# Two approximate 3x3 convolutions: channels ranked on chip, and softmax maxima in layer 2 for 3 of 11 channel groups

## The chip, the core and the metric

The kernel runs on one core of one Trainium2 chip. The metric is device microseconds of one execution. Before the change the median of three runs is 3927.82 us (3924.66 to 3930.93). One more execution was profiled. The engines are called as in the profile: PE is TensorE (PEld its weight loads), DVE is VectorE, ACT ScalarE, POOL GpSimd, SP SyncE.

## The reference

The input is 16 images of 256 channels with 28x28 pixels, all in fp32. For every image:

```python
g = group_norm(x)                       # 32 groups of 8 channels
h = relu(bn1(amm_conv3x3(g, centroids1, wsub1)))
y = bn2(amm_conv3x3(h, centroids2, wsub2))
y = y * sigmoid(relu(mean(y) @ se_w1 + se_b1) @ se_w2 + se_b2)
out = x + relu(y + g)

def amm_conv3x3(x, centroids, w_sub):   # centroids (256,16,9), w_sub (256,9,256)
    p = 3x3 patches of each channel                    # (b, n, c, s), s = 9
    d = sum(p*p) - 2 * einsum('bncs,cks->bnck', p, centroids) + sum(centroids**2)
    attn = softmax(-d, over the 16 codes k)
    lut = einsum('cks,cso->cko', centroids, w_sub)
    return einsum('bnck,cko->bno', attn, lut)
```

Each channel's 3x3 patch is softly replaced by a mix of 16 codes of nine numbers, and the mix, over all channels, goes through an ordinary product with `w_sub`. The term `p*p` is the same for all 16 codes and drops out of the softmax. What is left, the logit, is `2pc - cc`. In exact arithmetic the softmax doesn't depend on whether the largest logit is taken off ahead of the exponential; in fp32 a logit that is too large overflows, and a channel whose logits are all very negative loses its sum.

## The kernel before

**Tiling.** The 256 channels lie three to a *row tile* of 32 rows (9 patch rows each, and rows for other uses): 84 row tiles hold three channels, and four hold one of the last four each. Four row tiles fill the 128 partitions, and eight (two halves `h`) make one of 11 *groups*. Groups 9 and 10 come first, since their numbers are dealt out into spare rows of the other nine (`qx`, L503). The 784 pixels of an image are taken in two parts of 384 and 400. One group and one part is a *slot*: 22 slots make a *stage*, which is one layer of one image, and there are 32 stages in the order L1(0), L1(1), L2(0), L1(2), L2(1), and so on.

**What a slot does.** Patches `pt` come from a DRAM copy `pat` of the shifted image (L365, POOL's queue). TensorE forms 16 codes' logits for the 24 channels of the group with 16 products (L378, `wd` holds the codes and the term `cc`), ScalarE takes the exponential (L444), TensorE turns it into nine mixed numbers and one sum for each channel (L454, `cw`). VectorE turns these so that pixels lie on partitions (`nt`, L466) and takes reciprocals of the sums (`rc`, L470), POOL scales (L487, L493), VectorE turns back (`q`, L514), and TensorE forms the output products (L525, weights `ws`): 36 of 128x128 for each part, summed over nine groups in two accumulator banks. Layer 1 doesn't take maxima; it records the largest and smallest reciprocal of each slot instead (`ext`, L473 and L474).

**Maxima in layer 2.** Five slots ahead of its own, every slot of layer 2 forms the same logits once more. VectorE turns them (`z`, L397, two transposes) and takes the maximum over the 16 codes (`mx`, L405, two reductions), turns the result (`mt`, L414), and SP stores it to DRAM and loads it into four spare rows of `pt` (L423, L431), from where the later logit products subtract it. So these slots have two sets of L378 products and two DVE steps of each sort more.

**Order.** Every engine runs its instructions in the order in which they are written. The class `Plan` is a table: `at(slot, position, job)` files a job, and `emit` writes them sorted by slot and position. Within a slot the positions are: 0 logits for a maximum, 1 `z`, 2 `q`, 3 L454, 4 `nt`, `rc` and scaling, 5 logits, 6 exponential, 7 spare rows, 8 `mx`, 9 loading. A slot's own logits are in slot s, its L454 in s+1, its `q` in s+2, its output products from the fifth slot on. Output products are filed at position 1 or 7 (three or four of 36 in each slot; `early` in the code). Three pairs of PSUM banks (`pair`, 2 x 512 numbers) go around in the order of use; all logits and all L454 results share them.

**Side work** is filed into the same slots: the next image's norm on VectorE (`gn_stats` to `gn_apply`, L252 and L281), its shifted copies, the writing of the patches to DRAM (`to_pat`, L301, 15 transfers for a stage on ACT's queue), and the finish of the image before (SE gate, L351 to L353).

**The guard.** At the end the recorded reciprocals are tested. If a sum of exponentials left the range 1e-26 to 1e26 (`S_LIM`), a conditional block computes every image again with maxima in both layers.

The host only lays the arrays out (`wd`, `cw`, `ws` of both layers in row-tile order).

## Time and profile before

| | |
|---|---|
| median of three runs | 3927.82 us |
| profiled execution, its time | 3933.48 us |
| its span | 3931.8 us |
| PE busy | 91% of the span |
| DVE busy | 83% |
| ACT, POOL busy | 38%, 33% |
| mean granted clock of TensorE | 0.975 |
| chain that ended last | DVE 53%, PE 28% |

A group of the page names line, engine, operation, `out<-in` with the tiles' names, its count, its busy time and the mean of one, then the engine's idle time ahead of it and what ended most of that. A row of single instructions starts with its start time and its duration; `[1.60 <-POOL nt L487]` at its end says that the engine was idle for 1.60 us until POOL's result of line 487 came. The granted clock is TensorE's, as a share of full speed. A row of stretches gives start and end in us and, after the comma, the busy time of each engine inside it.

### The profile page before, as it was taken

The numbers are of one execution on the slowest core, as the hardware profiler recorded it, in microseconds if no ns is written. First come the engines' busy times: TensorE is split into PE (matmuls) and PEld (weight loads), VectorE is DVE, ScalarE is ACT, GpSimd is POOL, SyncE is SP. The second block draws the span as 40 slices with busy tenths as digits, with TensorE's granted clock in tenths as the row PEclk, the third lists the DMA queues.
The fourth block names the chain that finished last, engine by engine and source line by source line (L and its number), as shares of the span: only waits on it lengthen the run. The fifth ranks groups of instructions, "written<-read, shape, count | busy, mean of one in ns | idle before, by whom it ended". The sixth has DMA issues, their size and how long they took to land.

```text
span 3931.8 us, 81773 instructions
## 1 busy us (share of the span) xinstructions
PE 3570.4 (91%) x33042; PEld 1295.3 (33%) x33042; DVE 3261.3 (83%) x4710; ACT 1507.9 (38%) x2417; POOL 1283.9 (33%) x1314
## 2 busy tenths in 40 slices
...
GB/s 252 170 165 155 180 119 160 166 139 197 132 171 133 145 191 165 159 116 154 186 151 194 117 169 146 146 198 144 172 112 146 198 159 170 112 159 172 148 89 58
DMA packets 361805, 611.05 MB, mean 155 GB/s; under 512 B 205370, under 2 KB 217802, under 8 KB 361162
## 3 DMA queue, kind: packets, MB, share of 16 engines
...
HBM read 338.50 MB, written 271.94 MB: 155 GB/s over the span
## 4 chain that ended last, share of the span: by engine, by line
DVE 53%; PE 28%; issue 6%; DMA 5%; POOL 3%; ACT 2%; ACTq 2%; POOLq 0%; DVEq 0%; SPq 0%
PE acc L525 14%; DVE z L397 13%; DVE mx L405 11%; DVE nt L466 10%; DVE q L514 10%; PE pair L378 9%; DVE rc L470 5%; PE pair L454 5%; POOL nt L487 3%; ACTq L301 2%; DMA dm<-mt 1%; DMA pat<-side 1%; DVE y L352 1%; ACT y L351 1%; DVE y L353 1%
## 5 line engine op out<-in xcount | busy, mean ns | idle before, releaser
L444 ACT ACTIVATE e<-pair 128x768 f32<-128x768 f32 (+1 forms) x1408 | 1111.4, 822 | 1913.6 <-PE pair L378 1734.0
L525 PE MATMUL acc<-q,ws 128*128 128x384 f32 (+1 forms) x4608 | 1798.0, 523 | 0.0
L378 PE MATMUL pair<-pt,wd 31*64 31x400 f32 (+1 forms) x16896 | 1252.2, 519 | 246.1 <-DVE z L397 182.3
L487 POOL TENSOR_TENSOR nt<-nt,rc 128x648 f32<-128x648 f32 (+1 forms) x576 | 773.9, 1344 | 1752.5 <-DVE rc L470 1568.1
L525 PEld LDWEIGHTS acc<-q,ws 128*128 128x128 f32 x4608 | 818.4, 193 | 970.9 <-issue 582.4
L514 DVE STREAM_TRANSPOSE q<-nt 128x768 f32<-128x768 f32 (+1 forms) x576 | 569.0, 988 | 292.7 <-POOL nt L487 253.0
L466 DVE STREAM_TRANSPOSE nt<-pair 128x768 f32<-128x768 f32 (+1 forms) x704 | 688.8, 978 | 126.5 <-PE pair L454 123.6
L454 PE MATMUL pair<-e,cw 64*32 64x384 f32 (+1 forms) x11264 | 648.8, 506 | 76.0 <-DVE nt L466 61.6
L397 DVE STREAM_TRANSPOSE z<-pair 128x768 f32<-128x768 f32 (+1 forms) x704 | 665.5, 983 | 56.8 <-PE pair L378 55.6
L378 PEld LDWEIGHTS pair<-pt,wd 31*64 31x64 f32 x16896 | 310.8, 130 | 1114.9 <-DVE z L397 625.2
L405 DVE TENSOR_REDUCE mx<-z 128x48 f32<-128x768 f32 (+1 forms) x704 | 643.9, 957 | 0.0
L470 DVE RECIPROCAL rc<-nt 128x72 f32<-128x72 f32 (+1 forms) x704 | 438.2, 622 | 24.2
L365 POOL DMA_DIRECT2D pt<-pat x384 | 299.4, 780 | 446.2 <-PE pair L378 374.2
L503 ACT COPY nt<-qx 128x120 f32<-128x120 f32 (+1 forms) x576 | 183.8, 319 | 332.3 <-DVE rc L470 332.1
L493 POOL TENSOR_TENSOR qx<-nt,rc 128x324 f32<-128x324 f32 (+3 forms) x256 | 166.2, 668 | 407.7 <-DVE rc L470 396.3
L454 PEld LDWEIGHTS pair<-e,cw 64*32 64x32 f32 x11264 | 134.3, 105 | 476.8 <-issue 267.8
L352 DVE SCALAR_TENSOR_TENSOR y<-xt,gn_rstd,y 128x392 f32<-128x392 f32 x64 | 47.9, 749 | 77.6 <-ACT y L351 77.6
L473 DVE TENSOR_REDUCE ext<-rc 128x1 f32<-128x72 f32 (+1 forms) x352 | 81.3, 231 | 12.1
L414 DVE STREAM_TRANSPOSE mt<-mx 128x256 f32<-128x256 f32 x192 | 81.2, 423 | 6.5
L474 DVE TENSOR_REDUCE ext<-rc 128x1 f32<-128x72 f32 (+1 forms) x352 | 77.6, 220 | 0.0
L289 ACT COPY side<-im 128x756 f32<-128x756 f32 x64 | 52.6, 823 | 51.0 <-DMA pat<-im 35.9
L351 ACT ACTIVATE y<-y,se_nb,se_gt 128x392 f32<-128x392 f32 x64 | 45.3, 712 | 38.1 <-issue 34.3
...
## 6 DMA issues: line engine op xcount, KB each, us to landing
...
pat<-side ACTq DMA_DIRECT2D x128, 771.8 KB
...
```

Source lines behind the costliest of these rows:

```text
L365: nc.gpsimd.dma_start(pt[:, : 2 * len(gs), :n], view(u["pat"], 2 * gs[0] * P * HW + px, [[HW, P], [P * HW, 2 * len(gs)], [1, n]]),)
L378: nc.tensor.matmul(ps[i // 2][64 * h : 64 * h + 64, i % 2, :n], lhsT=wd[l][32 * i : 32 * i + rows, 2 * g + h, :], rhs=u["pt"][32 * i : 32 ...
L397: nc.vector.transpose(z[:, : 64 * nb].rearrange("p (i m) -> p i m", i=2), ps[:, :, : 32 * nb])
L405: nc.vector.tensor_reduce(u["mx"][:, a : a + 2].rearrange("p i (c b) -> p i b c", c=2)[:, :, :nb], z[:, : 64 * nb].rearrange("p (i b c k) ...
L444: nc.scalar.activation(e[:, :, :n], ps[:, :, :n], AF.Exp, scale=2.0)
L454: nc.tensor.matmul(ps[32 * i : 32 * i + 32, h, :n], lhsT=cw[l][64 * h : 64 * h + 64, g, i, :], rhs=es[i // 2][64 * h : 64 * h + 64, i % 2, ...
L466: nc.vector.transpose(t[:, : 2 * nb].rearrange("p (h b) r -> p h (b r)", h=2), u.pop(("nm", gi))[:, :, : 32 * nb])
L470: nc.vector.reciprocal(rc[:, : 2 * nb], t[:, : 2 * nb, SUM : SUM + 3])
L487: nc.gpsimd.tensor_tensor(v, v, rc[:, : 2 * nb].unsqueeze(3).to_broadcast([P, 2 * nb, 3, 9]), ALU.mult)
L503: nc.scalar.copy(u["nt", gi][0][:, : 2 * nb].rearrange("p (h b) r -> p h b r", h=2)[:, :, :, SUM:], bass.AP(w.tensor, w.offset, [list(w.ap ...
L514: nc.vector.transpose(q[:, : 64 * nb], t[:, : 2 * nb].rearrange("p b r -> p (b r)"))
L525: nc.tensor.matmul(accs[key][:, :n], lhsT=ws[l][:, 2 * g + h, o * P : (o + 1) * P], rhs=u["q", gi][:, 32 * nb * h : 32 * nb * h + n], star ...
```

## The change

The changed kernel takes maxima in layer 2 for groups 0, 3 and 6 only (`MAXED`). These three hold 72 channels, and which channels they are is found on the chip. At the start VectorE works out a key for each of the 256 channels between the layers, (5 |bn scale| + bn shift) times the largest sum of positive numbers of a code, and ranks the channels by it (`sort_channels`). The 72 highest go to the places of groups 0, 3 and 6 (`places`), the others follow. The rank makes a permutation matrix `perm`, and with it TensorE reorders all that has one entry for each of these channels: the outputs of layer 1 (`sort_bn`, `sort_ws1` in 18 blocks), and codes and weights of layer 2 (`sort_c2`, `sort_ws2` in six parts). The latter go to DRAM and from there by 86 transfers on SP's queue to their places in `wd`, `cw` and `ws` (`place_wd2`, `place_cw2`, `place_ws2`, `place_extra`). Layer 1 as computed then has its channels in sorted order, so layer 2 sees them so. All of that stands ahead of the plan's first slot.

In layer 2 the units are `MIXED`: four pairs of groups without maxima, and three single groups with them, whose patches have a pool of their own (`mpool`, three buffers; `ppool` has four instead of five). A group without maxima is treated as in layer 1, its range tests included, and its patches come four slots ahead instead of nine. Layer 2's logits are lowered by a constant 25 (`SHIFT`, through a row of ones in `pt`), and the limits of the guard become 1e-26 and 1e32. The conditional block still takes all maxima. Output products in a slot are split in two halves, position 1 and 7, where that slot has logits for a maximum, and all stand at position 7 elsewhere. The preparation of layer 2's codes (`setup_codes(1)`) moves from slot 4 to slot 18.

```diff
-S_LIM = 1e26
+S_MIN, S_MAX = 1e-26, 1e32
...
 ORDER = [9, 10] + list(range(NBG))
-UNITS = [ORDER[i : i + 2] for i in range(0, NG, 2)]
+PAIRS = [ORDER[i : i + 2] for i in range(0, NG, 2)]
+MAXED = (0, 3, 6)
+MIXED = [[9, 10], [0], [1, 2], [3], [4, 5], [6], [7, 8]]
+REACH = 5.0
+SHIFT = (0.0, 25.0)
...
+def places():
+
+    first = [rt + NFULL * j for g in MAXED for rt in range(8 * g, 8 * g + 8) for j in range(NCH)]
+    return first + [c for c in range(3 * NFULL + 4) if c not in first]
...
+    c2_sb = const.tile([P, NB, K * 9], F32, name="c2_sb")
+    nc.sync.dma_start(c2_sb, cent2.rearrange("(b p) m -> p b m", p=P))
+    sort_sb = hpool.tile([P, NB * HW], F32, tag="y", name="sort_sb")
+    n_in = sorting.shape[1]
+    nc.sync.dma_start(sort_sb[:, :n_in], sorting)
...
+    wd = [load(wd1, "wd0"), const.tile([P, NT, 64], F32, name="wd1")]
+    cw = [load(cw1, "cw0"), load(cw2, "cw1")]
+    ws = [const.tile([P, NBT, C], F32, name=f"ws{l}") for l in range(2)]
+    nc.gpsimd.memset(wd[1], 0.0)
...
-    NSTAT = B * len(PXT) * NG
+    NSTAT = B * len(PXT) * (2 * NG - len(MAXED))
...
+    def sort_channels():
+        sc, sh = bn[0]
+        key = small.tile([P, NB], F32, name="key")
+        pos = scratch(NB * K * 9)
+        nc.vector.tensor_scalar_max(pos, c2_sb.rearrange("p b m -> p (b m)"), 0.0)
+        sums = small.tile([P, NB * K], F32, name="sums")
+        nc.vector.tensor_reduce(sums, pos.rearrange("p (m s) -> p m s", s=9), axis=AX.X, op=ALU.add)
+        nc.vector.tensor_reduce(key, sums.rearrange("p (b k) -> p b k", k=K), axis=AX.X, op=ALU.max)
+        t = small.tile([P, NB], F32, name="key_t")
+        nc.vector.tensor_scalar_mul(t, sc, -1.0)
+        nc.vector.tensor_max(t, t, sc)
+        nc.vector.scalar_tensor_tensor(t, t, REACH, sh, op0=ALU.mult, op1=ALU.add)
+        nc.vector.tensor_mul(key, key, t)
+        ps = bank()
+        for b in range(NB):
+            dg = scratch(P)
+            nc.vector.tensor_scalar_mul(dg, ident, key[:, b : b + 1])
+            nc.tensor.matmul(ps[:, b * P : (b + 1) * P], lhsT=ones_sq, rhs=dg, start=True, stop=True)
+        row = scratch(C)
+        nc.vector.tensor_copy(row, ps[:, :C])
+        own = small.tile([P, NB], F32, name="key_own")
+        rank = small.tile([P, NB], F32, name="rank")
+        for b in range(NB):
+            dg = scratch(P)
+            nc.vector.tensor_mul(dg, row[:, b * P : (b + 1) * P], ident)
+            nc.vector.tensor_reduce(own[:, b : b + 1], dg, axis=AX.X, op=ALU.add)
+            gt = scratch(C)
+            eq = scratch(C)
+            nc.vector.tensor_scalar(gt, row, own[:, b : b + 1], None, op0=ALU.is_gt)
+            nc.vector.tensor_scalar(eq, row, own[:, b : b + 1], None, op0=ALU.is_equal)
+            nc.vector.tensor_mul(eq, eq, earlier[:, b])
+            nc.vector.tensor_add(gt, gt, eq)
+            nc.vector.tensor_reduce(rank[:, b : b + 1], gt, axis=AX.X, op=ALU.add)
+            nc.vector.tensor_scalar(perm[:, b], ranks, rank[:, b : b + 1], None, op0=ALU.is_equal)
...
+    PART = 384
+    def part_of(ap, i):
+        t = tpool.tile([P, 832], F32, tag="z", name="part")[:, : NB * PART].rearrange("p (b m) -> p b m", b=NB)
+        nc.sync.dma_start(t, ap[:, i * PART : (i + 1) * PART].rearrange("(b p) m -> p b m", p=P))
+        return t
+    def sort_ws1(i):
+        t = part_of(ws1, i)
+        for j in range(PART // P):
+            ps = bank()
+            for b in range(NB):
+                nc.tensor.matmul(
+                    ps[:, :C], lhsT=t[:, b, j * P : (j + 1) * P], rhs=perm[:, b], start=(b == 0), stop=(b == NB - 1)
+                )
+            nc.scalar.copy(ws[0][:, i * PART // P + j], ps[:, :C])
+    d_c2 = [dram.tile([C, K * 9], F32, name=f"dc2{i}") for i in range(2)]
+    d_ws2 = dram.tile([C, 9 * C], F32, name="dws2")
+    def by_position(ps, rhs, m):
+        for v in range(NB):
+            for b in range(NB):
+                nc.tensor.matmul(
+                    ps[:, v, :m], lhsT=perm[:, b, v * P : (v + 1) * P], rhs=rhs[:, b], start=(b == 0), stop=(b == NB - 1)
+                )
+    def sort_c2():
+        ps = pair()
+        by_position(ps, c2_sb, K * 9)
+        for i in range(2):
+            t = scratch(NB * K * 9).rearrange("p (b m) -> p b m", b=NB)
+            if i == 0:
+                nc.scalar.copy(t, ps[:, :, : K * 9])
+            else:
+                nc.scalar.copy(
+                    t.rearrange("p b (s k) -> p b s k", k=K), ps[:, :, : K * 9].rearrange("p b (k s) -> p b s k", s=9)
+                )
+            nc.scalar.dma_start(view(d_c2[i], 0, [[K * 9, P], [P * K * 9, NB], [1, K * 9]]), t)
+    def sort_ws2(i):
+        t = part_of(wsub2, i)
+        ps = pair()
+        by_position(ps, t, PART)
+        r = tpool.tile([P, 832], F32, tag="z", name="part")[:, : NB * PART].rearrange("p (b m) -> p b m", b=NB)
+        nc.scalar.copy(r, ps[:, :, :PART])
+        nc.scalar.dma_start(view(d_ws2, i * PART, [[9 * C, P], [P * 9 * C, NB], [1, PART]]), r)
+    def place_wd2(j, s):
+        r, m = prow(j, s), K * 9
+        nc.sync.dma_start(
+            wd[1][r::32, : NFULL // 4, K * j : K * j + K],
+            view(d_c2[1], NFULL * j * m + s * K, [[m, 4], [4 * m, NFULL // 4], [1, K]]),
+        )
...
+    dppool = ctx.enter_context(tc.tile_pool(name="ppool", bufs=5))
+    ppool = ctx.enter_context(tc.tile_pool(name="ppool", bufs=4))
+    mpool = ctx.enter_context(tc.tile_pool(name="mpool", bufs=3))
...
-        pt = ppool.tile([P, 4, 400], F32, tag="pt", name="pt")
+        if len(gs) > 1:
+            pt = ppool.tile([P, 4, 400], F32, tag="pt", name="pt")
+        else:
+            pt = mpool.tile([P, 2, 400], F32, tag="pm", name="pm")
...
+            for slot, looks in self.looks:
+                n = len(looks) // 2 if (slot, 0) in self.jobs else 0
+                for i, (g, o, h) in enumerate(looks):
+                    self.at(slot, 1 if i < n else 7, c_look, *g, o, h)
...
-                for ui, gs in enumerate(UNITS):
+                for gs in units:
+                    mx = gs[0] in maxed
...
-                        if maxed:
-                            at(s - LB, 0, a_logits, u, gi)
-                            at(s - LB, 1, a_turn, u, gi)
-                            at(s - LB, 8, a_max, u, gi)
+                        if mx:
+                            at(s - self.lb, 0, a_logits, u, gi)
+                            at(s - self.lb, 1, a_turn, u, gi)
+                            at(s - self.lb, 8, a_max, u, gi)
...
-                    at(n - LEAD - (LB if maxed else 0), 9, patches, u)
-                    if maxed:
-                        e = n + len(gs) - 1 - LB
+                    at(n - self.lead - (self.lb if mx else 0), 9, patches, u)
+                    if mx:
+                        e = n + len(gs) - 1 - self.lb
...
-                for k, (g, o, h) in enumerate(LOOKS):
-                    s, r = divmod(k * NG, len(LOOKS))
-                    early = maxed and 2 * r < len(LOOKS)
-                    at(n0 + LC + s, 1 if early else 7, c_look, *of[g], o, h)
+                    n += len(gs)
+                for s in range(NG):
+                    looks = [k for k in range(len(LOOKS)) if k * NG // len(LOOKS) == s]
+                    self.looks.append((n0 + LC + s, [(of[LOOKS[k][0]], *LOOKS[k][1:]) for k in looks]))
...
+    sort_channels()
+    sort_bn()
+    for i in range(NBT * P // PART):
+        sort_ws1(i)
+    sort_c2()
+    for i in range(9 * C // PART):
+        sort_ws2(i)
+    for j in range(NCH):
+        for s in range(9):
+            place_wd2(j, s)
+        for i in range(4):
+            for h in range(2):
+                place_cw2(h, i, j)
+            place_ws2(i, j)
+    for m in range(EXTRA // 9):
+        place_extra(m)
+    plan = Plan(4, 5)
...
-        plan.stage(l, b, pat_of(l, b), t, l == 1, cols if l == 0 else [])
+        plan.stage(l, b, pat_of(l, b), t, *((PAIRS, ()) if l == 0 else (MIXED, MAXED)), cols)
...
-    plan.at(4, 9, setup_codes, 1)
+    plan.at(18, 9, setup_codes, 1)
...
-    for i, (op, test, lim) in enumerate(((ALU.max, ALU.is_le, S_LIM), (ALU.min, ALU.is_ge, 1.0 / S_LIM))):
+    for i, (op, test, lim) in enumerate(((ALU.max, ALU.is_le, 1.0 / S_MIN), (ALU.min, ALU.is_ge, 1.0 / S_MAX))):
...
-            mones[32 * i + MROW[j], K * j : K * j + K] = -1.0
+            mones[:, 32 * i + MROW[j], K * j : K * j + K] = -1.0
+        for l in range(2):
+            mones[l, 32 * i + ONE] = -SHIFT[l] / 2
```

**How the instructions move.** Three places, in program order of one engine each; a tile's number only tells buffers apart.

VectorE before, inside a layer-2 stage: `q`, `nt` and `rc` of one slot, `mx` and `mt` of the maxima, `z` of the next:

```order
L514 STREAM_TRANSPOSE q<-nt 128x768
L466 STREAM_TRANSPOSE nt<-pair_79 128x768
L470 RECIPROCAL rc<-nt 128x72
L405 TENSOR_REDUCE mx_142<-z 128x2x12x2 x2
L414 STREAM_TRANSPOSE mt<-mx_142 128x128
L397 STREAM_TRANSPOSE z<-pair_79 128x832
L397 STREAM_TRANSPOSE z<-pair_80 128x832
L514 STREAM_TRANSPOSE q<-nt 128x768
```

The same place after (L572 is z, L580 mx, L589 mt, L641 nt, L645 rc, L648 and L649 the range tests, L689 q; L440 is a step of the next image's norm):

```order
L572 STREAM_TRANSPOSE z<-pair_79 128x768
L572 STREAM_TRANSPOSE z<-pair_80 128x768
L641 STREAM_TRANSPOSE nt<-pair_81 128x768
L645 RECIPROCAL rc<-nt 128x72
L580 TENSOR_REDUCE mx_147<-z 128x2x12x2 x2
L589 STREAM_TRANSPOSE mt<-mx_147 128x128
L440 TENSOR_TENSOR gn_var<-gn_gm,pair_81 128x2
L689 STREAM_TRANSPOSE q<-nt 128x768
L641 STREAM_TRANSPOSE nt<-pair_79 128x768
L645 RECIPROCAL rc<-nt 128x72
L648 TENSOR_REDUCE ext<-rc 128x1
L649 TENSOR_REDUCE ext<-rc 128x1
```

Before, z and mx stand in every slot; after, a slot with them is followed by slots that have only q, nt, rc and two range tests.

TensorE before, in a layer-2 stage (L378 logits, L525 output products, L454 mixing): two sets of logits in every slot:

```order
L378 MATMUL pair_80<-pt,wd_111 64x400 x4
L378 MATMUL pair_81<-pt,wd_111 64x400 x4
L525 MATMUL acc_13961<-q,ws_115 128x384 x2
L454 MATMUL pair_79<-e,cw_113 32x384 x8
L378 MATMUL pair_80<-pt,wd_111 64x400 x4
L378 MATMUL pair_81<-pt,wd_111 64x400 x4
L525 MATMUL acc_13996<-q,ws_115 128x384
L378 MATMUL pair_79<-pt,wd_111 64x400 x4
L378 MATMUL pair_80<-pt,wd_111 64x400 x4
```

After (L553 logits, L700 output products, L629 mixing; `pm` is the patch tile of a group with maxima):

```order
L553 MATMUL pair_81<-pm,wd_114 64x400 x4
L553 MATMUL pair_79<-pm,wd_114 64x400 x4
L700 MATMUL acc_12774<-q,ws_120 128x384 x2
L629 MATMUL pair_80<-e,cw_117 32x384 x8
L553 MATMUL pair_81<-pm,wd_114 64x384 x4
L553 MATMUL pair_79<-pm,wd_114 64x384 x4
L700 MATMUL acc_12771<-q,ws_120 128x384 x2
L629 MATMUL pair_80<-e,cw_117 32x384 x8
L553 MATMUL pair_81<-pt,wd_114 64x384 x4
L553 MATMUL pair_79<-pt,wd_114 64x384 x4
L700 MATMUL acc_12774<-q,ws_120 128x384 x2
L700 MATMUL acc_12771<-q,ws_120 128x384
```

A slot with maxima still has output products between its first logits and L629; in a slot without, all of them stand behind the one set of logits.

ScalarE at the start, before: the last patch transfers of image 0, then at once the first exponentials (L142 to L147 clear DRAM copies of patches):

```order
L301 DMA pat_82<-side_126 84x3x784
L301 DMA pat_82<-side_126 4x3x784
L444 ACTIVATE e<-pair_80 128x2x384
L444 ACTIVATE e<-pair_81 128x2x384
L142 DMA pat_84<-in_consts 352x1x784
L143 DMA pat_84<-in_consts 88x784
L147 DMA pat_84<-in_consts 4x3x784 x6
```

After, between these transfers and the first exponential (the end of `sort_ws1`, `sort_c2` and the start of `sort_ws2`):

```order
L326 COPY ws_119<-pair_81 128x256
L345 COPY scratch<-pair_79 128x288
L350 DMA dc_153<-scratch 128x2x144
L347 COPY scratch<-pair_79 128x288
L350 DMA dc_154<-scratch 128x2x144
L357 COPY part<-pair_80 128x768
L358 DMA dws_155<-part 128x2x384
L357 COPY part<-pair_81 128x768
L358 DMA dws_155<-part 128x2x384
```

The 18 copies of `sort_ws1` and the copies and stores of the sorted codes and weights stand between the patch transfers and the first exponential.

113 lines of the change are left out of this document (78 added, 35 removed).

## The prediction

> **What bounds the kernel now.** I read the page's totals first, then the busy time by stage, then single slots in order of time.
>
> ```profile
> PE 3570.4 (91%) x33042; PEld 1295.3 (33%) x33042; DVE 3261.3 (83%) x4710; ACT 1507.9 (38%) x2417; POOL 1283.9 (33%) x1314
> DVE 53%; PE 28%; issue 6%; DMA 5%; POOL 3%; ACT 2%; ACTq 2%; POOLq 0%; DVEq 0%; SPq 0%
> ```
>
> TensorE is busiest, yet VectorE holds 53% of the chain that ended last. These are averages over two kinds of slot, so I cut one pair of stages (layer 1 of image 9, layer 2 of image 8) at the first L454 matmul of a slot. In the rows below the columns are the stretch, its length, the busy time of PE, PEld, DVE, ACT, POOL, the granted clock, the DMA share and GB/s.
>
> ```profile
> 298.10:3629.60 3331.50, 3101.54 (x28904) 1126.90 (x28896) 2840.49 (x4089) 1319.67 (x2114) 1114.76 (x1135) 0.99 0.51 157
> 2090.79:2155.92 65.13, 61.91 (x587) 24.55 (x586) 45.35 (x84) 33.74 (x57) 28.12 (x31) 0.97 0.72 242
> 2155.92:2298.16 142.24, 130.27 (x1210) 44.82 (x1209) 135.66 (x182) 47.56 (x75) 41.66 (x43) 0.99 0.48 138
> 2303.56:2328.47 24.91, 24.91 (x235) 9.66 (x235) 16.66 (x21) 10.97 (x17) 9.46 (x8) 1.00 0.24 69
> ```
>
> The first row is 14 such pairs, 238.0 us each. The third is the 22 slots in which maxima are taken (five slots early, so seven of them lie in the layer-1 stage): 6.47 us a slot, DVE busy 95%. The second is 15 slots of layer 1 without maxima, 4.34 each, with patch writing and the previous image's finish in them. The last is six quiet slots of **layer 2** without maxima, because the early half has run out: 4.15 each. That is the case which the change makes common, already in the trace.
>
> A quiet slot, and what paces it:
>
> ```profile
> 2309.33 1.05 DVE L514 STREAM_TRANSPOSE q<-nt 128x832 f32<-128x832 f32 x1 [1.60 <-POOL nt L487]
> 2310.30 1.01 DVE L466 STREAM_TRANSPOSE nt<-pair 128x832 f32<-128x832 f32 x1
> 2311.34 0.64 DVE L470 RECIPROCAL rc<-nt 128x78 f32<-128x78 f32 x1
> ...
> 2312.09 0.91 PE L454 MATMUL pair<-e,cw 64*32 64x400 f32 x16
> 2312.15 1.40 POOL L487 TENSOR_TENSOR nt<-nt,rc 128x702 f32<-128x702 f32 x1 [2.86 <-DVE rc L470]
> 2312.93 0.93 PE L378 MATMUL pair<-pt,wd 31*64 31x400 f32 x16
> 2313.59 1.04 DVE L514 STREAM_TRANSPOSE q<-nt 128x832 f32<-128x832 f32 x1 [1.60 <-POOL nt L487]
> 2313.79 2.28 PE L525 MATMUL acc<-q,ws 128*128 128x400 f32 x6
> 2316.00 0.90 PE L454 MATMUL pair<-e,cw 64*32 64x400 f32 x16
> ```
>
> TensorE is packed: 3.91 us from L454 to L454 with three output products, one more product (0.76) in three of eleven slots. A second loop is just as long: transpose q, transpose nt, reciprocal, POOL's scaling, and q again, 2309.33 to 2313.59, 4.26 us; in it VectorE waits 1.60 for POOL. A slot with maxima:
>
> ```profile
> 2160.50 0.90 PE L378 MATMUL pair<-pt,wd 31*64 31x384 f32 x16
> 2161.33 0.90 PE L454 MATMUL pair<-e,cw 64*32 64x400 f32 x16
> 2161.44 1.85 DVE L397 STREAM_TRANSPOSE z<-pair 128x768 f32<-128x768 f32 x2 [1.36 <-PE pair L378]
> 2162.48 1.77 PE L378 MATMUL pair<-pt,wd 31*64 31x400 f32 x16 [0.24 <-DVE z L397]
> 2163.21 1.00 DVE L514 STREAM_TRANSPOSE q<-nt 128x832 f32<-128x832 f32 x1
> ...
> 2164.17 2.28 PE L525 MATMUL acc<-q,ws 128*128 128x400 f32 x6
> 2165.18 0.64 DVE L470 RECIPROCAL rc<-nt 128x78 f32<-128x78 f32 x1
> 2166.15 1.80 DVE L405 TENSOR_REDUCE mx<-z 128x48 f32<-128x768 f32 x2
> ```
>
> TensorE gives it 0.83 us (L378 to L454), VectorE 1.85 + 1.80.
>
> **The steady part, edit by edit.** Eight of eleven groups of layer 2 lose the first logits, z, mx and their share of mt and its DRAM round trip. They gain two range tests:
>
> ```profile
> L473 DVE TENSOR_REDUCE ext<-rc 128x1 f32<-128x78 f32 x176 | 41.2, 234 | 6.0
> L474 DVE TENSOR_REDUCE ext<-rc 128x1 f32<-128x78 f32 x176 | 39.3, 223 | 0.0
> L414 DVE STREAM_TRANSPOSE mt<-mx 128x128 f32<-128x128 f32 x32 | 10.0, 312 | 1.1
> L252 DVE BATCH_NORM_STATS2 gn_st<-xt 128x6 f32<-128x392 f32 x64 | 32.1, 544 | 10.1 <-DMA xt<-in_x 10.1
> L281 DVE TENSOR_SCALAR im<-xt,gn_gm,gn_rstd 128x784 f32<-128x784 f32 x32 | 24.1, 796 | 1.2 <-POOL gn_rstd L208 1.2
> ```
>
> The tests, 0.234 + 0.223 = 0.46, fit into VectorE's 1.60 wait for POOL and cost nothing; without that cover they would cost 16 x 0.46 = 7.3 us a stage. So a stage without maxima is 22 x 4.15 = 91.3.
>
> Six slots a stage keep maxima, each followed by at least two without. What does one add? At least TensorE's 0.83. At most what a crowded one adds today, 6.47 - 4.15 = 2.31. My value comes from the VectorE-POOL loop: z (1.85) can start after the range test, so 0.46 + 1.85 = 2.31 stand where the wait was 1.60, +0.7; after the next reciprocal 0.46 + 1.80 + 0.31 = 2.57 stand there, +1.0. POOL is then no longer late: the next nt is, and with it the PSUM pair that L454 writes two slots on, where TensorE, 0.83 later itself, waits about 1.0. Both give 1.7 to 1.9; I take **1.85**. The split of the output products, which now goes by slot, puts one or two of them between the first logits and L454, so the transposes stay covered on TensorE's side.
>
> Layer 2 also carries the next image's norm, 4 x 0.54 + 2 x 0.80 = 3.8 on VectorE, and patch writing on ACT. Hidden today under full slots, they now meet slots of 4.15. Layer 1's fifteen show what such side work costs: 65.13 - 15 x 4.15 = 2.9. I take 4 for layer 2 (bounds 0 and 2.9 + 3.8 = 6.7).
>
> A pair: layer 1, 65.13 + 7 x 4.15 = 94.2; layer 2, 91.3 + 6 x 1.85 + 4 = 106.4; together **200.6**, against 238.0. Bounds: 190.5 (0.83 and no side cost) and 206.1 (2.31 and 6.7). The new buffers, four pairs and three singles, cost nothing: a pair lives six slots, a single nine, and POOL's issue finds one free.
>
> **The start.** The sort is in front of everything.
>
> ```profile
> 0.00:72.25 72.25, 7.31 (x28) 3.74 (x28) 11.49 (x39) 5.23 (x7) 11.24 (x21) 0.70 0.78 270
> 72.25:176.10 103.85, 93.11 (x840) 34.95 (x843) 69.56 (x120) 43.39 (x68) 39.99 (x42) 0.92 0.59 189
> 176.10:298.10 122.00, 106.22 (x960) 38.98 (x960) 81.59 (x135) 44.75 (x71) 41.56 (x42) 0.96 0.50 156
> 3629.60:3782.40 152.80, 135.77 (x1213) 44.81 (x1205) 134.18 (x164) 45.41 (x72) 38.80 (x39) 0.92 0.43 123
> 3782.40:3931.80 149.40, 126.39 (x1121) 45.90 (x1120) 124.03 (x167) 49.47 (x86) 37.52 (x37) 0.95 0.25 70
> 28.40:72.25 43.85, 1.59 (x16) 0.36 (x16) 0.26 (x2) 3.95 (x6) 3.03 (x4) 0.50 0.71 235
> 69.78 1.59 PE L378 MATMUL pair<-pt,wd 31*64 31x384 f32 x16 [44.22 <-DMA pt<-pat]
> 50.01 7.85 ACTq L301 DMA_DIRECT2D pat<-side  x5
> pt<-pat POOLq DMA_DIRECT2D x32, 384.0 KB, 3.9
> L431 SPq DMA_DIRECT2D pt<-dm x384: 502/563/1952, 275.4 to 3888.0; - x192
> ```
>
> VectorE's ranking (some 30 small operations) ends before ACT is free, so it costs nothing; ACT issues patches until 57.9 and its sorting copies stand behind that. TensorE can run three of layer 1's 18 weight blocks ahead, one for each PSUM pair; each of the other 15 is four half products of 256 columns. By the 2.28 for six half products of 400, one of 256 takes 0.25 and one of 384 takes 0.37 at full clock. In this window the granted clock was 0.50, and the first 16 logit matmuls took 1.59 instead of 0.90, 1.77 times as long. Cold, the 15 blocks take 60 x 0.44 = 26.4, to 84.3, and the codes 2. Layer 2's six weight parts use three buffers, in and out in turn: the load of a part waits for the store of the part two before. Per two parts that is load 3.9 (the 384 KB row, the nearest in size), eight half products of 0.66, copy 0.8, store 3.9, so 13.9; the first two are loaded early (10.6). The end: 86.3 + 10.6 + 2 x 13.9 = 124.7, first L454 2.5 later at 127. At full clock the same sum gives 57.9 + 15 + 1 + 6 + 2 x 11.6 + 2.5 = 106. I take **117** instead of 72.25, between them, as TensorE is idle in some of these waits and dense in others.
>
> The Trainium skill (TensorE: Matmul & The Clock Gate, "Part 1: The HAM clock gate") says that TensorE falls to half rate after an idle window of about 3.4 us. By that rule the waits for loads and stores would keep the sort cold, and the total would be 10 us higher. The 0.50 after the idle start agrees; no row here shows the sort itself.
>
> Then 86 placing transfers go through SP. At the L431 median, 0.563 us, they need 48 us, ahead of layer 2's preparation in slot 18, which is 18 x 4.15 = 75 us off. ACT's clearing and patch transfers share completion semaphores with them in the build, so some exponentials are late: I add 5 to stage 0 (bounds -5 and the third rival).
>
> **The sum**, in the profiled execution's time: start 117; stage 0, 103.85 + 5 = 108.9; stage 1, 122.0 - 7 x 2.31 + 1.85 = 107.7; 14 pairs x 200.6 = 2808.4; the next stage (layer 2 of image 14, 22 crowded slots), 152.8 - 22 x 2.31 + 6 x 1.85 = 113.1; the last with its tail, 149.4 - 15 x 2.31 + 5 x 1.85 = 124.0. Span **3379** against 3931.8. The execution was 1.7 longer than its span and 5.7 above the median of three, which leaves **3375** as a median.
>
> **Rivals.**
>
> First: VectorE stays the bound and a slot with maxima costs its full 2.31, with all side work showing: a pair of 206.1, 14 x 5.5 = 77 more, 3452. For it: VectorE at 95% in the crowded stretch; against: two or more slots without maxima follow each, where it has 1.60 idle. Chance 0.17.
>
> Second: TensorE alone sets the pace, all VectorE work fits and preparation hides: pairs of 190.5, 14 x 10.1 = 141 less, 3234. For it: the quiet row, PE busy 24.91 of 24.91; against: the loop of 4.26 beside TensorE's 3.91. Chance 0.14.
>
> Third: placing starves ACT. If its small pieces go at L431's slowest, 1.95, the 86 need 168 us, 93 beyond slot 18; POOL stands there in layer 2's code preparation and all scaling queues behind it: 3468. For it: each waits for an earlier transfer; against: the median is 0.563. Chance 0.09.
>
> Fourth, the slower side: the range test at the end fails and the conditional block computes every image again with all maxima. It decides if any unmaxed sum of exponentials leaves 1e-26 to 1e32. Price: 16 images x 44 crowded slots x 6.47 = 4555 more, some 7900. The reference's inputs, evaluated through its formulas with this ranking, give sums between 10^-15.9 and 10^26.4 outside the three groups, so the margin is wide; 46 of 256 channels do pass 10^32 somewhere, and all lie in the three groups. Chance 0.03.
>
> Fifth: the change doesn't shorten slots, since something other than maxima makes them long; then only the start's 45 shows, 3970, or about 3930 where small savings cover it. The quiet layer-2 slots speak against it. Chance 0.02.
>
> **The numbers.** My forecast, 3300 to 3440, has 0.55. The range has to take in most of the first two rivals: low 3240, high 3480. A difference of 0.2% (8 us) is what these runs can tell from none. Faster: 0.55 + 0.17 + 0.14 + 0.09 = 0.95; slower: the fourth and half of the fifth, 0.04; the same: the other half, 0.01.
>
> **What would show it.** In the changed profile: z and mx groups 192 instead of 704; first L454 near 117; pairs of 200.6, quiet slots in layer 2 near 4.15 throughout, slots with maxima near 6.0; VectorE's wait for POOL before q gone after those slots, and L454 two slots on waiting for nt. VectorE busy near 3261 - 512 x (0.98 + 0.96) + 256 x 0.46 = 2386, so 70% of the span. I am wrong if the quiet slots of layer 2 run above 4.5, if a pair differs from 190 to 206, or if the start passes 135.

## The result and the profile after

The changed kernel takes 3376.84 us (median of four runs) against 3929.38 before (four executions here, three above): a ratio of 0.8586, 95% interval 0.8557 to 0.8615. Predicted were 3375. The agreement is closer than the working deserves: the terms were off by up to 33 us each, and that the errors cancel is luck. One execution of all those below was slow, 4154.08 us at a granted clock of 0.658: the ratios leave it out, but it is one of the four behind the median of 3281.29 us given for the start in the plan, which is 3278.33 without it. First the profile, then the terms.

Busy time and the chain that ended last, from the page of the changed kernel (its L553 is the old L378, L629 is L454, L641 nt, L689 q, L700 the output products, L619 the exponential):

```profile
PE 3123.8 (92%) x29086; PEld 1220.5 (36%) x29086; DVE 2441.5 (72%) x4132; ACT 1477.0 (44%) x2443; POOL 1305.4 (39%) x1347
PE 42%; DVE 31%; DMA 12%; POOL 6%; issue 4%; ACT 3%; ACTq 2%; SPq 0%; POOLq 0%; DVEq 0%
L572 DVE STREAM_TRANSPOSE z<-pair 128x768 f32<-128x768 f32 (+1 forms) x192 | 184.0, 995 | 59.1 <-PE pair L553 59.0
L580 DVE TENSOR_REDUCE mx<-z 128x48 f32<-128x768 f32 (+1 forms) x192 | 177.8, 969 | 0.0
```

The instructions of z and of mx are down from 704 each to 192 each, as said. VectorE's busy time fell by 820 us and TensorE's by 447; TensorE now holds more of the chain than VectorE. Not all of the 447 is work taken away: 4096 fewer logit products make 213 at 0.83 us for 16. Most of the rest, by estimate, is time in which the other logit products stood half done behind z, which the profile counts as busy: in the groups of the two pages one takes 74 ns of TensorE's busy time before and 61 after. The stretches, cut at the first L629 of a stage as the prediction cut them (columns as there: stretch, length, PE, PEld, DVE, ACT, POOL, clock, DMA share, GB/s):

```profile
0.00:111.70 111.70, 54.10 (x172) 35.73 (x173) 19.87 (x69) 17.36 (x33) 12.44 (x22) 0.80 0.64 205
111.70:254.00 142.30, 98.01 (x837) 35.60 (x838) 67.70 (x120) 42.43 (x68) 39.95 (x42) 0.80 0.57 151
254.00:355.90 101.90, 95.42 (x880) 36.18 (x880) 66.00 (x114) 43.42 (x70) 40.34 (x41) 0.98 0.52 163
355.85:3142.30 2786.45, 2668.42 (x25313) 1032.62 (x25312) 2117.99 (x3557) 1281.15 (x2114) 1132.85 (x1162) 0.99 0.55 178
3142.30:3249.90 107.60, 101.57 (x950) 37.44 (x950) 80.87 (x125) 43.94 (x72) 39.61 (x40) 0.97 0.49 157
3249.90:3379.10 129.20, 106.32 (x949) 42.98 (x948) 89.12 (x151) 48.70 (x87) 40.24 (x40) 0.93 0.26 85
```

| term of the sum | predicted | measured | difference |
|---|---|---|---|
| start | 117 | 111.7 | -5 |
| stage 0 | 108.9 | 142.3 | +33 |
| stage 1 | 107.7 | 101.9 | -6 |
| 14 pairs | 14 x 200.6 = 2808 | 14 x 199.0 = 2786 | -22 |
| next stage | 113.1 | 107.6 | -6 |
| last, with its tail | 124.0 | 129.2 | +5 |

So there are two questions for the experiments: what a pair of 199.0 is made of, since 14 of them are the gain, and what makes stage 0 long. Who keeps TensorE waiting in the 14 pairs of the kernel before (total us, times, longest):

```profile
PE pair L378 <- DVE z L397: 165.8, 252, 1.9
PE pair L454 <- DVE nt L466: 56.1, 61, 3.2
```

and in those of the changed kernel (L427 is the product for the next image's mean):

```profile
PE pair L629 <- DVE nt L641: 65.9, 91, 3.0
PE pair L629 <- ACT e L619: 26.3, 14, 2.9
PE pair L427 <- DVE nt L641: 19.6, 14, 1.6
```

and what VectorE waits for in the latter (L520 and L505 are steps of the finish, each behind ScalarE's step on the same tile; L420 is the first step of the next image's norm):

```profile
DVE q L689 <- POOL nt L662: 332.7, 268, 1.8
DVE nt L641 <- PE pair L629: 100.3, 59, 4.5
DVE y L520 <- ACT y L519: 72.7, 56, 3.9
DVE z L572 <- PE pair L553: 45.6, 44, 3.2
DVE se_gt L505 <- ACT se_gt L502: 39.2, 14, 3.5
DVE gn_st L420 <- DMA xt<-in_x: 15.5, 14, 1.4
```

### The profile page after: what moved, and what is told of

Same layout as the page of the kernel before. It is cut to its first block, busy times and chain, and to the rows that moved or that the text cites. A ratio compares the mean times of both kernels' runs of the same rounds, so it can differ in the third digit from the quotient of the medians.

```text
span 3379.1 us, 72223 instructions
## 1 busy us (share of the span) xinstructions
PE 3123.8 (92%) x29086; PEld 1220.5 (36%) x29086; DVE 2441.5 (72%) x4132; ACT 1477.0 (44%) x2443; POOL 1305.4 (39%) x1347
## 4 chain that ended last, share of the span: by engine, by line
PE 42%; DVE 31%; DMA 12%; POOL 6%; issue 4%; ACT 3%; ACTq 2%; SPq 0%; POOLq 0%; DVEq 0%
PE acc L700 21%; PE pair L553 10%; DVE nt L641 9%; DVE q L689 8%; PE pair L629 8%; POOL nt L662 6%; DVE rc L645 5%; DMA pm<-dm 3%; DVE mx L580 3%; DMA xt<-in_x 2%; ACTq L469 2%; DVE z L572 2%; DMA dm<-mt 2%; DVE y L520 1%; ACT y L519 1%
## 5 line engine op out<-in xcount | busy, mean ns | idle before, releaser
L700 PE MATMUL acc<-q,ws 128*128 128x384 f32 (+1 forms) x4608 | 1740.5, 513 | 0.0
L619 ACT ACTIVATE e<-pair 128x768 f32<-128x768 f32 (+1 forms) x1408 | 1084.4, 821 | 1382.0 <-PE pair L553 1138.8
L700 PEld LDWEIGHTS acc<-q,ws 128*128 128x128 f32 x4608 | 814.8, 190 | 920.0 <-issue 483.1
L689 DVE STREAM_TRANSPOSE q<-nt 128x768 f32<-128x768 f32 (+1 forms) x576 | 575.6, 999 | 431.1 <-POOL nt L662 381.5
L641 DVE STREAM_TRANSPOSE nt<-pair 128x768 f32<-128x768 f32 (+1 forms) x704 | 690.7, 981 | 220.3 <-PE pair L629 217.9
L629 PE MATMUL pair<-e,cw 64*32 64x384 f32 (+1 forms) x11264 | 666.3, 509 | 147.1 <-ACT e L619 78.4
L553 PE MATMUL pair<-pt,wd 31*64 31x384 f32 (+1 forms) x9216 | 566.9, 519 | 2.7 <-DVE z L572 1.5
L645 DVE RECIPROCAL rc<-nt 128x72 f32<-128x72 f32 (+1 forms) x704 | 438.4, 623 | 24.2
L629 PEld LDWEIGHTS pair<-e,cw 64*32 64x32 f32 x11264 | 141.6, 105 | 544.5 <-ACT e L619 265.8
L553 PEld LDWEIGHTS pair<-pt,wd 31*64 31x64 f32 x9216 | 148.2, 131 | 397.4 <-issue 320.2
L538 POOL DMA_DIRECT2D pt<-pat x288 | 228.2, 793 | 39.7 <-DMA pat<-side 37.9
L553 PE MATMUL pair<-pm,wd 31*64 31x384 f32 (+1 forms) x3584 | 219.9, 527 | 8.8 <-DVE nt L641 4.5
L572 DVE STREAM_TRANSPOSE z<-pair 128x768 f32<-128x768 f32 (+1 forms) x192 | 184.0, 995 | 59.1 <-PE pair L553 59.0
L580 DVE TENSOR_REDUCE mx<-z 128x48 f32<-128x768 f32 (+1 forms) x192 | 177.8, 969 | 0.0
L648 DVE TENSOR_REDUCE ext<-rc 128x1 f32<-128x72 f32 (+1 forms) x608 | 140.5, 231 | 20.9
L649 DVE TENSOR_REDUCE ext<-rc 128x1 f32<-128x72 f32 (+1 forms) x608 | 134.1, 221 | 0.0
L553 PEld LDWEIGHTS pair<-pm,wd 31*64 31x64 f32 x3584 | 55.5, 132 | 148.1 <-issue 83.3
L520 DVE SCALAR_TENSOR_TENSOR y<-xt,gn_rstd,y 128x392 f32<-128x392 f32 x64 | 47.9, 749 | 75.5 <-ACT y L519 75.5
L538 POOL DMA_DIRECT2D pm<-pat x128 | 93.0, 726 | 0.0
```

Of the source, the lines that this page charges most:

```text
L538: nc.gpsimd.dma_start(pt[:, : 2 * len(gs), :n], view(u["pat"], 2 * gs[0] * P * HW + px, [[HW, P], [P * HW, 2 * len(gs)], [1, n]]),)
L553: nc.tensor.matmul(ps[i // 2][64 * h : 64 * h + 64, i % 2, :n], lhsT=wd[l][32 * i : 32 * i + rows, 2 * g + h, :], rhs=u["pt"][32 * i : 32 ...
L572: nc.vector.transpose(z[:, : 64 * nb].rearrange("p (i m) -> p i m", i=2), ps[:, :, : 32 * nb])
L580: nc.vector.tensor_reduce(u["mx"][:, a : a + 2].rearrange("p i (c b) -> p i b c", c=2)[:, :, :nb], z[:, : 64 * nb].rearrange("p (i b c k) ...
L619: nc.scalar.activation(e[:, :, :n], ps[:, :, :n], AF.Exp, scale=2.0)
L629: nc.tensor.matmul(ps[32 * i : 32 * i + 32, h, :n], lhsT=cw[l][64 * h : 64 * h + 64, g, i, :], rhs=es[i // 2][64 * h : 64 * h + 64, i % 2, ...
```

## The experiments

All edits are against the changed kernel, and each was timed beside the kernel before. Where a pair is given, it is the time from the third to the 31st stage of the profiled execution, over 14.

**All maxima back.**

```diff
-MAXED = (0, 3, 6)
-MIXED = [[9, 10], [0], [1, 2], [3], [4, 5], [6], [7, 8]]
+MAXED = tuple(ORDER)
+MIXED = PAIRS
...
-    ppool = ctx.enter_context(tc.tile_pool(name="ppool", bufs=4))
-    mpool = ctx.enter_context(tc.tile_pool(name="mpool", bufs=3))
+    ppool = ctx.enter_context(tc.tile_pool(name="ppool", bufs=5))
```

> Undoes one part alone: all 11 groups of layer 2 take maxima again, in pairs and with five patch buffers; ranking, reordering and placing stay. My theory: the maxima alone made the pairs shorter, so a pair is back at 238 (before: 238.0), and the whole is that of before plus what the start and stage 0 gave up in the changed kernel (39 + 38): about 4005. Rival, the other edits (patches four slots ahead, output products split by slot) carry part of the gain: pairs of 233 or less, below 3935.

Measured: 4004.29 us, ratio 1.0178 (1.0157 to 1.0198). The 14 pairs:

```profile
374.44:3705.87 3331.43, 3123.67 (x28898) 1116.46 (x28897) 2839.41 (x4089) 1316.54 (x2114) 1114.21 (x1134) 0.98 0.51 157
```

3331.43 / 14 = 237.96; before it was 3331.50 / 14. So ranking, reordering and placing change nothing in the pairs, and all of the gain there goes with the maxima. The rival wasn't tested apart: with the maxima this run also takes back what the plan ties to them, patches nine slots ahead, five buffers, and output products split in two halves in 22 slots of a pair instead of six. What speaks against it is that TensorE waits for patches in the 14 pairs of neither kernel. Ranking, reordering and placing by themselves cost 1.8% of the time before.

**No maxima.**

```diff
-MAXED = (0, 3, 6)
-MIXED = [[9, 10], [0], [1, 2], [3], [4, 5], [6], [7, 8]]
+MAXED = ()
+MIXED = PAIRS
```

> Layer 2 without any maxima: no group has its logits formed twice, all units are pairs. The logits are scaled by 0.1 instead of 2 in layer 2's exponential, so that nothing overflows, and the guard's limits are opened: the numbers are others, and the time shows the program without its 96 maxima slots (16 images, 6 each). My theory: a maxima slot adds 1.85 us (a pair of stages goes from 199.0 to 187.9, the whole from 3377 to about 3199). Rival, TensorE alone pays: 0.83 us a slot, a pair of 194.0, about 3297. Rival, VectorE pays all of its work: 2.31 us a slot, a pair of 185.1, about 3155.

Measured: 3257.18 us, 0.828 (0.825 to 0.8311). The 14 pairs, and eleven quiet slots in a row with one full round of the output products (from the 13th slot of a layer-1 stage on):

```profile
339.26:3035.87 2696.61, 2560.39 (x23970) 1010.97 (x23969) 1836.91 (x3305) 1272.95 (x2114) 1113.17 (x1134) 0.98 0.56 181
1837.80:1882.44 44.64, 44.64 (x424) 17.32 (x424) 31.43 (x54) 20.82 (x33) 20.99 (x21) 1.00 0.36 115
```

A quiet slot is 44.64 / 11 = 4.06 us, and TensorE is busy in all of it. A pair is 192.6, so six maxima slots cost 6.4, 1.07 each (over slots that have range tests instead): between my 1.85 and the 0.83 of TensorE's products alone. From this I formed the theory that only TensorE pays, and tested it with the next run.

**The maxima's reductions twice.**

```diff
-        for v, z in enumerate(u.pop(("z", gi))):
+        for v, z in list(enumerate(u.pop(("z", gi)))) * 2:
```

> The changed kernel with both maximum reductions of a maxima slot done twice: 1.8 us more of VectorE's work in each of 96 slots, nothing more for TensorE. The prediction's way of pricing (what VectorE does beyond POOL's wait lengthens the loop and TensorE waits for nt two slots on): all of it shows, 6 x 1.8 = 10.9 a pair, 210, the whole about 3550. The theory from the run without maxima (1.07 us a slot, near TensorE's 16 logit products, 0.98 by the groups' mean): VectorE has room in the slots that follow and makes it good there, the pair rises by 0 to 3, the whole stays below 3425.

Measured: 3508.92 us, 0.8935 (0.8909 to 0.8962), a pair 207.3. The 14 pairs:

```profile
351.86:3254.20 2902.34, 2687.80 (x25314) 1040.98 (x25313) 2267.89 (x3725) 1283.05 (x2114) 1132.58 (x1162) 0.99 0.53 171
```

and TensorE's wait for nt in them:

```profile
PE pair L629 <- DVE nt L641: 190.2, 164, 3.0
```

The theory fell: 8.3 us a pair came, where it allowed 3 and the prediction's pricing said 10.9. VectorE's work rose by 2267.89 - 2117.99 = 150 us, the time by 116, and TensorE's wait for nt by 190.2 - 65.9 = 124. Where it shows up is seen from slot to slot. The table, worked out from the traces, has the mean time from L629 to the next slot's L629, in the first eleven slots of layer 2, over 14 stages. Counted so, the first logits of the six maxima stand in the slots 2, 7, 10 and 13 of layer 2 and 18 and 21 of layer 1.

```
slot          1     2     3     4     5     6     7     8     9    10    11
no maxima  4.52  8.42  6.05  3.85  4.42  3.77  3.77  4.49  3.80  3.77  3.91
changed    4.55  7.38  4.15  4.06  4.42  3.77  6.12  3.13  4.31  6.22  3.25
mx twice   6.27  6.13  4.02  6.86  4.45  3.77  6.12  3.13  6.16  6.34  3.62
```

The clean place is the slots 7 to 9: a maxima slot makes them 13.56 us long instead of 12.06, 1.50 more. Of this 0.99 lies in the slots 7 and 8, where TensorE has 16 logit products more, and 0.51 in slot 9, two slots on. The doubled reductions leave 7 and 8 alone and put the full 1.85 on 9. That is the step of the prediction, the next nt late and L454 (now L629) two slots on behind it.

The mean over all six places came out lower (1.07) since in slots 2 to 4, where the next image's norm stands, the stages without maxima are slower, 18.3 against 15.6. The trace of the run without maxima shows why (its L626 is L629, L638 nt, L426 the product for the next image's mean, L419 the norm's first step):

```profile
PE pair L426 <- DVE nt L638: 56.8, 14, 5.1
DVE gn_st L419 <- DMA xt<-in_x: 58.6, 14, 5.3
```

VectorE waits 58.6 us in the 14 pairs for the next image's input, against 15.5 in the changed kernel, and TensorE's product for the mean waits behind it, 56.8 against 19.6. That is 2.7 a pair, all of the difference in slots 2 to 4. In the traces this load is issued 2.7 us after the first slot's L629 and lands 6.4 us later; in the changed kernel it is 1.7 and 4.9. Why the load comes later was not tested. With these 2.7 us set aside, six maxima slots cost 9.1, 1.5 each, as at the clean place.

**No range tests in layer 2** (the guard then covers layer 1 only).

```diff
-                        "groups": gs, "maxed": mx, "col": [None if mx else cols.pop() for _ in gs],
+                        "groups": gs, "maxed": mx, "col": [None if mx or l else cols.pop() for _ in gs],
```

> The two range tests of a reciprocal are left out in layer 2 (256 slots), so the guard covers layer 1 only. My theory: they stand in VectorE's wait for POOL and cost nothing, so a pair stays within 1 us of 199.0 and the whole within 0.4% of 3377. Rival, they lengthen the loop of VectorE and POOL: 16 x 0.46 = 7.3 us a pair, about 117 in all, 3260.

Measured: 3329.58 us, 0.8465 (0.8449 to 0.8481), a pair 196.1:

```profile
348.15:3093.62 2745.47, 2657.44 (x25314) 1034.87 (x25313) 2035.20 (x3109) 1277.16 (x2114) 1135.21 (x1162) 0.99 0.56 181
```

Between the two theories: 2.9 a pair of the 7.3 show. Not in the quiet slots of layer 2 (3.90 with and without, in slots 17 and 18), but where it also writes patches: the 12th slot falls from a mean of 6.66 to 4.69, the 13th from 6.51 to 5.91. In the changed kernel's trace VectorE waits 1.2 us for POOL before q in the 17th slot, and not at all in the 12th and 13th.

**The finish of an image, split.** Its steps on VectorE, and those of the gate ahead of it, stand one slot behind ScalarE's (the lines show the finish alone).

```diff
-                    self.at(te + 3 + 2 * k + i, 9, finish, b, k, i)
+                    self.at(te + 4 + 2 * k + i, 9, finish, b, k, i)
+                    self.at(te + 5 + 2 * k + i, 9, finish2, b, k, i)
```

> VectorE's half of the gate and of the finish of an image is filed one slot behind ScalarE's half (both stood at the same place). My theory: the side work costs more than I had taken since VectorE stands still for ScalarE in it (72.7 + 39.2 us over the 14 pairs, 8 a pair), and TensorE's waits for nt follow from that; a pair falls by 3 to 6, the whole to 3290 to 3335. Rival: VectorE has that much slack, TensorE's waits come from elsewhere, and the pair stays within 1 of 199.0.

Measured: 3321.45 us, 0.8447 (0.8417 to 0.8477), a pair 194.6:

```profile
355.37:3079.91 2724.54, 2654.15 (x25314) 1029.34 (x25313) 2164.73 (x3557) 1277.76 (x2114) 1141.94 (x1162) 1.00 0.56 182
```

with TensorE's wait for nt in them (L637 is L629, L649 nt):

```profile
PE pair L637 <- DVE nt L649: 13.0, 53, 0.4
```

VectorE's work is no less (2164.73), yet 4.4 a pair are gone, and TensorE's wait for nt falls from 65.9 to 13.0. In the changed kernel 55 of these 65.9 us lay in layer 1's slots 10 to 13; the slots 8 to 12 took 25.9 together and now take 21.1. VectorE's two waits for ScalarE, 72.7 and 39.2 us, are no longer in its list. So this was the larger part of layer 1's side work: not work, but VectorE standing still for ScalarE inside it.

**The norm, three slots later.**

```diff
-            for k, f in enumerate((gn_stats, gn_mean, gn_var, gn_apply)):
+            for k, f in zip((2, 4, 5, 6), (gn_stats, gn_mean, gn_var, gn_apply)):
...
-            plan.prep(0, pat_of(0, b), t - NS + 5, False)
+            plan.prep(0, pat_of(0, b), t - NS + 8, False)
```

> The four steps of the next image's norm are filed into slots 3, 5, 6 and 7 of a layer-2 stage instead of 1 to 4 (its patches three slots later). My theory: the second slot of layer 2, 7.4 us where a slot with maxima takes 6.1 elsewhere, pays for the input that lands late and for TensorE's product that waits for it (19.6 us in the pairs); the pair falls by about 2, the whole to about 3345. Rival: it is the sum of VectorE's work that counts and not its place: the same time shows up in the later slots, the whole within 8 of 3377.

Measured: 3377.30 us, 0.8587 (0.8558 to 0.8616), a pair 199.3. A miss, and the rival was right: the second slot falls from 7.4 to 5.6, and what it lost is back in the fourth, eighth, 15th and 16th.

**Patches written by SP.**

```diff
-        nc.scalar.dma_start(
+        nc.sync.dma_start(
             view(pat, (32 * rt + base) * HW, [[32 * HW, n], [step * HW, 3], [1, HW]]),
```

> The transfers that write the patches (15 a stage) are issued by SP instead of ScalarE. My theory of what is left over in a pair, 199.0 against some 190.6 of TensorE's busy time: part of it is ScalarE sitting in these issues (148 us over the 14 pairs wait for pat), which makes exponentials late; TensorE itself waits 26.3 us for them in the pairs, so at least 26 and up to 60 us are gained, and a pair falls to 195 to 197. Rival: the stores and loads of the maxima, which share SP's queue, come late instead, and a pair is 199 or longer.

Measured: 3347.81 us, 0.8507 (0.8478 to 0.8536), a pair 197.2. The gain, 29 us, is at the low end of what was said, and the rival is partly right: TensorE's waits for exponentials fall from 78.4 us in the whole execution to 35.2, but patches come late instead.

```profile
PE pair L629 <- DVE nt L641: 43.3, 81, 1.6
PE pair L553 <- DMA pt<-pat: 37.0, 25, 3.1
PE pair L629 <- ACT e L619: 35.2, 5, 17.8
PE pair L553 <- DMA pm<-pat: 26.2, 14, 4.0
```

**Stage 0.** ScalarE in the first slots of the changed kernel (ACTq rows are its issue of transfers, here those that clear a DRAM copy of patches):

```profile
111.76 0.80 ACTq L163 DMA_DIRECT2D pat<-in_consts  x1
112.60 15.99 ACTq L167 DMA_DIRECT2D pat<-in_consts  x6
128.63 1.51 ACT L619 ACTIVATE e<-pair 128x768 f32<-128x768 f32 x2 [16.32 <-DMA cw<-dc]
...
134.29 0.79 ACTq L163 DMA_DIRECT2D pat<-in_consts  x1
135.12 16.62 ACTq L167 DMA_DIRECT2D pat<-in_consts  x6
151.85 1.51 ACT L619 ACTIVATE e<-pair 128x768 f32<-128x768 f32 x2 [17.08 <-DMA pat<-in_consts]
```

The same six transfers in the kernel before, in its first and third slot with nothing on SP's queue, and at its very start beside SP's loads of codes and weights:

```profile
73.21 4.05 ACTq L147 DMA_DIRECT2D pat<-in_consts  x6
83.22 6.06 ACTq L147 DMA_DIRECT2D pat<-in_consts  x6
3.39 22.89 ACTq L147 DMA_DIRECT2D pat<-in_consts  x6
```

In the trace each of these issues first waits until an earlier transfer on its completion semaphore has landed, and SP's transfers use the same eight semaphores. The wait of 16.32 us ends with a placing transfer of SP (`cw<-dc`). In the second six, 9.6 us are a wait for ScalarE's own first clearing transfer of that slot: with SP's transfers in the round, its turn came back to that semaphore while the transfer was still on its way.

The first run was to spread the placing over slots 6 to 30.

```diff
+    for i, job in enumerate(placing):
+        plan.at(6 + i // 3, 9, *job)
-    plan.at(18, 9, setup_codes, 1)
+    plan.at(36, 9, setup_codes, 1)
```

> The 86 placing transfers no longer stand in one block ahead of the plan: three calls of them are filed into each of slots 6 to 30, and the preparation of layer 2's codes goes from slot 18 to 36. My theory: stage 0 is 142.3 us long instead of 109, since ScalarE's transfers of clear_pat queue behind SP's placing, and the exponentials with them; spread out, stage 0 falls to about 110 and the whole by 30, to about 3347. Rival, what makes stage 0 long is the bandwidth that small pieces take, or a cold TensorE clock: stage 0 and 1 together stay at 244, the whole within 8 of 3377.

Measured: 3366.65 us, 0.8561 (0.8546 to 0.8576), stage 0 131.4. Inconclusive: SP has nothing in its program that waits for a slot, so it issued the first placing at 103.34 us, as in the changed kernel at 102.32, and the two long waits stayed (18.7 and 18.4). Of the 10.9 us that stage 0 lost, 6.7 are the codes' preparation, which now stands in stage 1. The second run takes the clearing off ScalarE.

```diff
     def clear_pat(i):
         t = d_pat[i]
+        eng = nc.scalar if i == 0 else nc.gpsimd
...
-        nc.scalar.dma_start(view(t, 7 * HW,
+        eng.dma_start(view(t, 7 * HW,
```

> The clearing of the two other DRAM patch copies (16 transfers in slots 0 and 2) is issued by POOL instead of ScalarE; the placing transfers stay. My theory: in stage 0 ScalarE sits 16 us twice in this issue, since its transfers wait for completions of SP's placing, and TensorE waits for the exponentials behind it; so the slots of 17.8 and 18.6 us fall below 6, stage 0 goes from 142 to about 115, the whole to about 3350. Rival: the small pieces fill the DMA engines, and whoever waits for patches or codes waits as long: stage 0 stays above 130.

Measured: 3360.59 us, 0.8541 (0.8513 to 0.8568). The start and stage 0:

```profile
0.00:117.16 117.16, 53.39 (x169) 34.71 (x169) 19.86 (x69) 17.34 (x33) 17.38 (x30) 0.81 0.66 210
117.16:234.87 117.71, 92.61 (x834) 34.17 (x835) 67.25 (x120) 43.02 (x68) 44.95 (x50) 0.90 0.63 169
```

Stage 0 falls from 142.3 to 117.7, with the placing as it was: that ScalarE issued the clearing beside it made some 25 of the 33. No run takes the placing away and leaves the clearing with ScalarE, so that SP is what ScalarE stands behind rests on the waits in the trace. The start is 5.5 longer; POOL issues the first clearing in it (from 68.6 us on), while TensorE waits for weight parts, but that the one makes the other wasn't shown.

**What follows, put together.** On top of the split finish, first the start: the sorting of layer 2's weights moved into the slots (not shown: SP clears the other two patch copies, and the codes are prepared in four pieces).

```diff
-    for i in range(9 * C // PART):
-        sort_ws2(i)
...
+    for i in range(9 * C // PART):
+        plan.at(1 + 2 * i, 9, load_ws2, i)
+        plan.at(3 + 2 * i, 8, sort_ws2, i)
+    for job in placing:
+        plan.at(14, 9, *job)
```

> e10's split of the finish, and the start taken apart: the six parts of layer 2's weights are loaded and sorted in slots 1 to 13 instead of ahead of the plan, the placing stands behind them, the other two patch copies are cleared by SP, and layer 2's codes are prepared in four pieces in slots 31 to 36. My theory: the weight parts hold the start from 74 to 109 us, of which only TensorE's 6 x 3.0 are work; the first L454 comes at 77, stage 0 takes 94 + 18 + some 5 for side work = 117 instead of 143, so layer 1 of image 1 begins at 194 instead of 256, pairs stay at 194.6, the whole about 3255. Rival: the loads and stores only move, and slots 3 to 13 wait for them as the start did: stage 0 at 140 or more, the whole 3290 or more.

Measured: 3281.29 us, 0.8346 (0.8324 to 0.8369).

```profile
0.00:76.47 76.47, 30.64 (x120) 23.25 (x120) 19.87 (x69) 12.53 (x27) 12.42 (x22) 0.91 0.75 244
76.47:191.34 114.87, 104.20 (x874) 41.83 (x875) 64.73 (x115) 47.26 (x74) 36.98 (x38) 0.96 0.73 197
191.34:300.92 109.58, 98.72 (x889) 38.05 (x888) 70.21 (x119) 43.49 (x70) 43.27 (x45) 0.97 0.61 181
```

Start and stage 0 are as expected (77 and 117). Stage 1 gave 10 us back, in slots in which ScalarE again waits for transfers while SP places weights (one of 7.5 us for `ws`), and the pairs at 195.5 instead of 194.6 make another 12.

> As c1, with the 15 patch transfers of a stage going in turn through ScalarE's and SP's issue. My theory: half of ScalarE's wait for them is gone while SP isn't held up as with all of them, so a pair falls by 1.5 to 4 against c1. Rival: what the transfers wait for is the completion of earlier ones on either engine, and ScalarE waits as long as in c1: within 0.7 of its pair.

```diff
-        nc.scalar.dma_start(
+        (nc.sync if i % 2 and in_plan else nc.scalar).dma_start(
             view(pat, (32 * rt + base) * HW, [[32 * HW, n], [step * HW, 3], [1, HW]]),
```

With the patches on two queues on top: 3283.42 us, 0.8361 (0.8337 to 0.8385), a pair 195.1 against 195.5. The rival was right on the time, not on the reason: ScalarE's waits for `pat` in the pairs fell from 152 to 61, but layer 2's 13th slot takes 9.3 instead of 6.4.

> As c1, with the range tests as two sums on ScalarE (sum of the reciprocals, sum of the sums; both are bounds on the largest) instead of a maximum and a minimum on VectorE. My theory, after the run without layer 2's tests (47 us for 256 of 608 pairs of tests): VectorE is the later engine where side work lies, so a pair falls by 3 against c1, the whole by 40 to 80. Rival: ScalarE is the later one there, and two more instructions ahead of its exponentials cost as much as VectorE gains: within 10 of c1, or slower.

```diff
-            nc.vector.tensor_reduce(ext[:, 0, col : col + 1], rc[:, : 2 * nb], axis=AX.XY, op=ALU.max)
-            nc.vector.tensor_reduce(ext[:, 1, col : col + 1], rc[:, : 2 * nb], axis=AX.XY, op=ALU.min)
...
+        nc.scalar.activation(
+            junk[:, : 2 * nb], t[:, : 2 * nb, SUM : SUM + 3] if i else rc[:, : 2 * nb], AF.Identity,
+            scale=1.0, accum_out=ext[:, i, col : col + 1],
+        )
```

The range tests on ScalarE, on top of the start in the plan: 3230.21 us, 0.8226 (0.8202 to 0.8251), the fastest. It leaves nothing out: a sum of positive numbers under a limit keeps each of them under it. A pair is 191.9:

```profile
304.84:2990.86 2686.02, 2645.00 (x25314) 1029.16 (x25313) 1960.55 (x2493) 1594.25 (x4243) 1157.20 (x1162) 1.00 0.57 185
```

TensorE is busy in 98.5% of it, in the changed kernel in 95.8%, though ScalarE has a quarter more to do.

## Why the prediction was right, and where it was wrong

**The bound.** Right. Slots without maxima run as the six quiet slots of the kernel before did: 4.06 us over eleven slots (ten of them in layer 1) against the 4.15 read from six; in the same run layer 2's last seven slots take 28.6 us, 4.09 each. 44 x 0.09 = 4 us a pair of the difference is that reading; six slots held a little more than their share of output products.

**The maxima slot, 1.85.** The mechanism was right, the size was within its bounds: 1.50 at the clean place. TensorE's part came out about as said (0.99 for 0.83); the wait two slots on, put at about 1.0, measured 0.51. That VectorE's work is what sets it is shown by the doubled reductions, which come out in full at that slot. As 6 x 1.85 = 11.1 the term was 4.7 too large for the 6.4 that a pair lost: 2.0 by this size, and 2.7 because the stages without maxima wait longer for the next image's input, which the forecast didn't have.

**Range tests at no cost.** Wrong. VectorE's wait for POOL covers them in a quiet slot, but the slots of layer 2 that write patches have no such wait; 2.9 a pair, some 47 us in all. The price without cover was given as 7.3.

**Side work, 2.9 + 4.** Wrong in size and in kind. Without maxima a pair is 192.6 - 44 x 4.06 = 14.0 above its quiet slots, twice what I took; the tests are in it, and 4.1 of TensorE's wait behind the next image's input (56.8 / 14). I had priced it by VectorE's instructions; the larger part of layer 1's was VectorE waiting for ScalarE (4.4 a pair went when the order alone was changed).

So in the pair 182.6 + 11.1 + 6.9 = 200.6 was forecast, and 178.6 + 6.4 + 14.0 = 199.0 came: three terms off by 4 to 7 us, and by luck a sum off by 1.6. VectorE's busy time, 2386 in the forecast, is 2441.5; z and mx fell by 948 us where 993 were reckoned.

**The start.** 111.7 for 117. Layer 1's blocks and the codes ended at 73.8, the sum at full clock (57.9 + 15 + 1), not the cold one of 86.3. The weight parts took 35.6 from there to the first logits at 109.45, between the 38.4 cold and the 29.2 warm; the granted clock was 0.75 in it (the stretch):

```profile
76.65:109.45 32.80, 22.71 (x48) 12.20 (x48) 0.00 (x0) 4.00 (x5) 0.00 (x0) 0.75 0.37 111
```

and the parts in it, two by two, behind their loads:

```profile
76.65 6.86 PE L334 MATMUL pair<-part,sort_sb 128*128 128x384 f32 x16 [2.82 <-DMA part<-in_wsub]
88.48 7.77 PE L334 MATMUL pair<-part,sort_sb 128*128 128x384 f32 x16 [4.96 <-DMA part<-in_wsub]
```

Its 0.75 is a mean. The clock fell to 0.50 around each wait and rose to 1.00 inside each block of products, as the stretches of the second block show:

```profile
86.44:93.27 6.83, 4.79 (x8) 2.70 (x9) 0.00 (x0) 0.00 (x0) 0.00 (x0) 0.50 0.40 126
93.27:100.10 6.83, 2.98 (x10) 1.43 (x8) 0.00 (x0) 1.60 (x2) 0.00 (x0) 1.00 0.43 108
```

The rule that the prediction took from the Trainium skill (TensorE: Matmul & The Clock Gate, "Part 1: The HAM clock gate"), half rate after an idle window, agrees with the falls. That the waits would keep the sort cold was the prediction's own step from it, and it failed: the clock was full again 4.8 us after the second block began (88.48 to 93.27).

**Stage 0, +5.** Wrong by 33: this is the third rival's place, ScalarE's transfers behind SP's placing, but not its price. The 86 placing transfers, put at 48 us, took 110 (102.3 to 212.9). It didn't reach the codes' preparation in slot 18 (that slot took 10.6). It struck in the first and third slot, 17.8 and 18.6 us where the kernel before had 5.9 and 8.0, and again where ScalarE writes patches while SP still places (one wait of 9.35 us for `cw<-dc`, one of 8.03 for `pat<-side`). I had seen that the two share completions and priced it at 5.

**The other rivals.** VectorE staying the bound at 206.1 a pair: no, though VectorE is so near to it that of 1.8 more in each maxima slot three quarters show (8.3 of 10.9 a pair). TensorE alone at 190.5: not the changed kernel, but the last version comes within 1.4 of it. The conditional block didn't run. The slots did shorten.
